# A triangle multiplication and a gated pair layer on one core: opening, first pair and drain laid out anew

## The chip, the cores and the metric

The kernel runs on one core of a Trainium2 chip, in one launch. The metric is the device time of a whole execution in microseconds. Engines are called by their short names: PE (TensorE, matmuls and transposes), DVE (VectorE), ACT (ScalarE), POOL (GpSimd) and SP (the queue from which most transfers are issued).

## The reference

x is 384 x 384 x 128 in fp32. Two layers follow each other; `_linear(x, W, b)` multiplies by the transposed W and adds b.

```python
# layer 0
z_n = _layernorm(z, norm_g, norm_b)
a = _linear(z_n, Wa, ba) * sigmoid(_linear(z_n, Wga, bga))
b = _linear(z_n, Wb, bb) * sigmoid(_linear(z_n, Wgb, bgb))
x = einsum('bijd,bjkd->bikd', a, b)
x = _layernorm(x, normo_g, normo_b)
z = z + _linear(x, Wo, bo) * sigmoid(_linear(z_n, Wgo, bgo))
# layer 1, with pair = z
left = pair @ W_left + b_left + (pair @ W_eq + b_eq)
right_sum = sum(pair @ W_right + b_right, axis=2)
gate = sigmoid(pair @ W_gate + b_gate)
out = (left * right_sum * gate) @ W_out + b_out
result = layer_norm(out + pair) * ln_scale + ln_bias
```

## The kernel before

The work goes in three stages.

**Stage 1** (about 0 to 1396 us) makes a, b and the output gate. It runs over 72 tiles n of 128 rows by 16 columns, each in four steps of four columns (`TS` is 4), 288 steps in all. A step s (`step`, L227) puts on PE the projections pga, pa, pgb, the transposes ptr of the next step (`turn`, L174), pb and the gate products pgo. ACT normalises columns to zn (L160), copies the transposed columns to zT (L191) and takes sigmoids; DVE takes the statistics of later columns (L141, L142) and forms at, bt and gs; POOL forms the factors of the norm (`norm_factors`, L144, whose power is L149), adds the bias to x for the residual (`residual`, L171) and issues the stores of a, of the gate and of the residual (A, G and Z in DRAM).

The opening stands ahead of the first step (L335 to L378). The first tile of x is fetched in four parts, the weights of layer 0 are fetched on ACT's queue (`weight`, L292), and `prepare` (L297) makes each weight ready: PE transposes it (L300), DVE copies it (raw, L302) and scales it by norm_g (L304), and a product of raw with norm_b is added to the bias (L309, L310, or L306, L307 for the gate of the output, "go"). `first_quarter` and `normalise` work on the first tile four columns at a time. `last_weights` (L313) prepares the weight of the output and a few constants of layer 1; it is a generator that goes one piece further after each step from s = `CATCH_UP`, which is 12.

The last columns of b stay in SBUF as b_held and are stored to B in pieces at the beginning of stage 2 (`store_held`, L539).

**Stage 2** (about 1396 to 2147 us) forms, for each of 128 channels d and three blocks ib of 128 rows, the product pm of a and b over 384 (`multiply`, L549, L554). Five of these products are begun early (`EARLY`, L577), before the last third of b is there. For each product DVE subtracts the first channel (xd, L566), ACT squares, DVE sums the squares (L547), POOL sums xd (L573), and SP stores xd into X. The last eight channels (`LAST`) are held in SBUF and run block by block, so that the deviation of one block (`deviation`, L455, a generator: variance, root, reciprocal, one Newton step, and `turn_factors` at L480) can go on beside the products of the next block. In the last block, `layer_0` is done for the rows u = 0 and 1 behind the third-last and the second-last product.

**Stage 3** (about 2147 to 3331 us) goes over the 384 rows u. The order within a turn of the loop is written out as a tuple of stages, each with a lag in rows: load, gate_product 3, turn 2, out_weights 7, layer_1 8, layer_0 0, norm_factors 12, normalise 13, project 2, last_right 2, store 17. Four rows (`R`) share a group: one norm of layer 1 on POOL and one store. A row puts on PE py (L437), ptr (L632), pleft and pg (L684, L686) and pf (L658); pf needs h from DVE and w_o, which is W_out scaled on ACT by the sums of that row (L640). The deviation of the last block runs on POOL beside the first rows (`last_deviation`, L485). The last rows pass through the same stages with nothing behind them; the store of the last eight is scaled on DVE (L709, L710) and issued row by row.

PSUM has eight banks; in stage 3 py, pf and pleft have two each, ptr and pg one each.

Of the kernel before, what the change touches and what calls it, by code (L numbers as in the profile page):

```python
# [1 line left out]

# [17 lines left out]
def kernel(ctx: ExitStack, tc: tile.TileContext, ins, out: bass.AP):  # L20
# [82 lines left out]
    with tc.tile_pool(name="wprep", bufs=6) as wp, tc.tile_pool(name="p1s", bufs=3) as ps, tc.tile_pool(  # L103
# [40 lines left out]
        def norm_factors(n, c0=0, c1=CX):  # L144
            if n >= NT:
                return
            mv, rstd, off = (tiles[n][k][:, c0:c1] for k in ("mv", "rstd", "off"))
            nc.gpsimd.tensor_scalar(rstd, mv[:, :, 1], EPS, None, ALU.add)
            nc.gpsimd.tensor_tensor(rstd, rstd, mhalf[:, 0 : c1 - c0], ALU.pow)  # L149
            nc.gpsimd.tensor_tensor(off, mv[:, :, 0], rstd, ALU.mult)  # L150
            nc.gpsimd.tensor_scalar(off, off, -1.0, None, ALU.mult)  # L151
            if c0 == 0:
                tiles[n]["zn"] = px.tile([P, CX, C], FP, tag="zn", name=f"zn_{n}", bufs=2)
# [20 lines left out]
        def turn(s):  # L174
# [4 lines left out]
            for c in range(CT):  # L179
                nc.tensor.transpose(ptr[:, c, :], tiles[n]["zn"][:, t * CT + c, :], ident)  # L180
            turned[s] = ptr
# [115 lines left out]
        def prepare(k):  # L297
            both = ppp.tile([P, CT, P], FP, tag="pk", name="w_" + k)
            pt, pb = both[:, 0, :], both[:, 1, :]
            nc.tensor.transpose(pt, wT[k], ident)  # L300
            raw = wp.tile([P, P], FP, tag="raw", name="raw_" + k, bufs=2)
            nc.vector.tensor_copy(raw, pt)  # L302
            scaled = ctile([P, P], "wT_" + k)
            nc.vector.tensor_scalar(scaled, raw, ng, None, ALU.mult)  # L304
            if k == "go":
                nc.tensor.matmul(pb, lhsT=nb_w, rhs=raw, start=True, stop=True)  # L306
                nc.vector.tensor_tensor(gate_bias, pb, gate_bias, ALU.add)  # L307
            else:
                nc.tensor.matmul(pb[:, 0:1], lhsT=raw, rhs=nb, start=True, stop=True)  # L309
                nc.vector.tensor_tensor(bcol[k], pb[:, 0:1], bcol[k], ALU.add)  # L310
            wT[k] = scaled

        def last_weights():  # L313
# [3 lines left out]
            pt = ppp.tile([P, CT, P], FP, tag="pk", name="pt_o")[:, 0, :]  # L317
            nc.tensor.transpose(pt, wT["o"], ident)
            raw, scaled = (wp.tile([P, P], FP, tag="raw", name=k + "_o", bufs=2) for k in ("raw", "scaled"))
            nc.vector.tensor_copy(raw, pt)  # L320
            nc.vector.tensor_scalar(scaled, pt, og, None, ALU.mult)
# [6 lines left out]
            nc.tensor.matmul(both[:, 1, :], lhsT=ob_w, rhs=raw, start=True, stop=True)  # L328
# [9 lines left out]
        for k in ("ga", "a", "gb", "b", "go"):  # L338
            weight(k, nc.scalar)
        nc.scalar.activation(warm, mhalf, AF.Sigmoid)  # L340
        ng, nb = column(L0 + "norm_g"), column(L0 + "norm_b")
        for k in ("ga", "a", "gb", "b"):
            bcol[k] = column(L0 + "b" + k)
            if k in ("a", "b"):
                next(x_parts)
# [18 lines left out]
        first_quarter(0)  # L364
        normalise(0, 0)
        prepare("ga")
        prepare("a")
        turn(0)
        turned_out(0)
        first_quarter(1)  # L370
        normalise(0, 1)
        prepare("gb")
        prepare("b")
        first_quarter(2)
        nc.vector.tensor_copy(nb_w, nb.to_broadcast([P, P]))
        prepare("go")
        first_quarter(3)
        later = last_weights()  # L378
        for s in range(NT * TS):
            step(s)  # L380
            if s >= CATCH_UP:
                next(later, None)
# [72 lines left out]
    def deviation(ib):  # L455
# [4 lines left out]
        v, t, r, sg, sd = (work(k) for k in ("v", "t", "r", "sg", "sd"))  # L460
# [7 lines left out]
        yield  # L468
        nc.scalar.activation(t, r, AF.Square)
# [4 lines left out]
        nc.vector.tensor_tensor(sd, v, r, ALU.mult)  # L474
        nc.sync.dma_start(out=X[ib][0], in_=sd)
# [8 lines left out]

    def last_deviation(ib, bank):  # L485

        v, t, r = (work_of.tile([P, N], FP, tag="w" + k, name=f"{k}_{ib}") for k in "vtr")
# [23 lines left out]
    with tc.tile_pool(name="p2", bufs=1, side="right", reuse_waits="tile") as p2, tc.tile_pool(  # L511
# [11 lines left out]
        order = [d for k in range(C // HELD) for d in range(k, C, C // HELD)]  # L523
# [15 lines left out]
        def store_held(i):  # L539
            if i < C:  # L540
                k = i // HELD
                nc.sync.dma_start(out=B[k :: C // HELD, N - P :, N - CG :], in_=b_held[k :: C // HELD])
# [37 lines left out]
        store_held(0)  # L580
# [4 lines left out]
        store_held(HELD)  # L585
        for d, ib in EARLY:
            multiply(d, ib, range(NB - 1))
        for d in range(C - LAST):
            fetch(d + AHEAD)
            if (d + 2) % HELD == 0:  # L590
                store_held(d + 2 + HELD)
# [8 lines left out]
        behind = None  # L600
        for ib in range(NB):
            for d in range(C - LAST, C):
# [8 lines left out]
                if ib == NB - 1 and d in (C - 3, C - 2):  # L611
                    layer_0(d + 3 - C, -1, lambda u: pp2.tile([P, N], FP, tag="pm", name=f"py_{u}").rearrange(
                        "p (q c) -> p q c", q=NB
                    ))
            add_squares()
            behind = deviation(ib) if ib < NB - 1 else None
# [4 lines left out]
    with tc.tile_pool(name="p3s", bufs=4, reuse_waits="tile") as ps, tc.tile_pool(  # L621
        name="p3g", bufs=4, reuse_waits="tile"
    ) as pg3, tc.tile_pool(name="p3y", bufs=2, space=PSUM, reuse_waits="tile") as pyp, tc.tile_pool(
        name="p3p", bufs=1, space=PSUM, reuse_waits="tile"
    ) as pp:
        hs, wos = {}, {}

        def turn(u):
            g, i = of(u)
            ptr = pp.tile([P, N], FP, tag="ptr", name=f"ptr3_{u}")  # L630
            for q in range(NB):
# [137 lines left out]
```

## Time and profile before

| What | us |
|---|---|
| Median of 3 runs | 3332.29 (3332.16 to 3332.49) |
| Profiled execution, its own time | 3332.67 |
| Its span, first to last instruction | 3330.9 |
| PE busy | 3289.1 (99%) |
| DVE busy | 2661.4 (80%) |
| ACT busy | 2309.9 (69%) |
| POOL busy | 2178.3 (65%) |
| Step of stage 1, usual period | 4.77 |
| Row of stage 3, usual period | 3.00 |

All times in the text are microseconds from the beginning of the span of this one execution, unless a line says otherwise. In lines of the timeline the first number is the start and the second the duration; a group in brackets at the end tells how long the engine stood idle before the instruction and what ended that.

### The profile page before, as it was taken

The numbers are of one execution on the slowest core, as the hardware profiler recorded it, in microseconds if no ns is written. First come the engines' busy times: TensorE is split into PE (matmuls) and PEld (weight loads), VectorE is DVE, ScalarE is ACT, GpSimd is POOL, SyncE is SP. The second block draws the span as 40 slices with busy tenths as digits, with TensorE's granted clock in tenths as the row PEclk, the third lists the DMA queues.
The fourth block names the chain that finished last, engine by engine and source line by source line (L and its number), as shares of the span: only waits on it lengthen the run. The fifth ranks groups of instructions, "written<-read, shape, count | busy, mean of one in ns | idle before, by whom it ended". The sixth has DMA issues, their size and how long they took to land.

```text
span 3330.9 us, 53440 instructions
## 1 busy us (share of the span) xinstructions
PE 3289.1 (99%) x15581; PEld 2188.5 (66%) x15581; DVE 2661.4 (80%) x8593; ACT 2309.9 (69%) x5485; POOL 2178.3 (65%) x1628
## 2 busy tenths in 40 slices
PE   8999999999999999999999999999999999999997
PEld 5555555555555555555555555588888888888885
DVE  8877777777777777555555555799999999999998
ACT  7777778787878788622222222388888888888887
POOL 6555555555555555355555555579999988888887
PEclk9999999999999999999999999999999999999998
DMA  6889899888988888899999999767777777777773
GB/s 224 266 256 273 277 281 281 280 276 281 285 275 270 256 273 279 276 347 310 318 312 311 312 312 304 262 238 266 266 264 261 261 260 262 262 264 263 262 264 143
DMA packets 675523, 910.52 MB, mean 273 GB/s; under 512 B 319521, under 2 KB 616481, under 8 KB 647713
## 3 DMA queue, kind: packets, MB, share of 16 engines
q1 hardware_dynamic: 634192, 680.28, 63.2%
q0 software_dynamic: 40320, 226.51, 19.4%
q8 instruction: 126, 2.06, 0.2%
q14 instruction: 165, 1.34, 0.1%
q10 hardware_dynamic: 720, 0.33, 0.0%
HBM read 454.04 MB, written 452.98 MB: 272 GB/s over the span
## 4 chain that ended last, share of the span: by engine, by line
PE 97%; DVE 1%; POOL 1%; ACT 0%; DMA 0%; issue 0%; POOLq 0%; ACTq 0%; DVEq 0%
PE pm L554 22%; PE py L437 8%; PE pf L658 8%; PE pga L246 8%; PE pleft L684 7%; PE pg L686 7%; PE pa L246 7%; PE pgb L246 7%; PE pb L246 7%; PE pgo L211 7%; PE ptr L632 4%; PE ptr L180 4%; PE pg L697 0%; DMA G<-gt 0%; POOL rs L667 0%
## 5 line engine op out<-in xcount | busy, mean ns | idle before, releaser
L554 PE MATMUL pm<-ab 128*128 128x384 f32 x2304 | 744.1, 486 | 1.5 <-DVE gs L213 1.5
L554 PEld LDWEIGHTS pm<-ab 128*128 128x128 f32 x2304 | 437.3, 190 | 306.4 <-DVE gs L213 2.7
L573 POOL TENSOR_TENSOR acc<-acc,xd 128x384 f32<-128x384 f32 x381 | 380.6, 999 | 362.7 <-DVE xd L566 362.7
L571 ACT ACTIVATE sq<-xd 128x384 f32<-128x384 f32 x381 | 188.5, 495 | 545.6 <-DVE xd L566 545.5
L276 DVE SCALAR_TENSOR_TENSOR bt<-pb,c_L_conv_bb,sgb 128x512 f32<-128x512 f32 x288 | 320.6, 1113 | 244.1 <-ACT zT L191 218.8
L160 ACT ACTIVATE zn<-xt,off,rstd 128x128 f32<-128x128 f32 x1152 | 503.3, 489 | 2.9 <-POOL off L151 2.8
L676 ACT ACTIVATE res<-res,off,rs 128x128 f32<-128x128 f32 x1152 | 482.3, 486 | 14.3 <-POOL off L670 11.4
L566 DVE TENSOR_TENSOR xd<-pm,acc 128x384 f32<-128x384 f32 x381 | 212.1, 557 | 340.9 <-POOL acc L573 321.3
L267 POOL DMA_DIRECT2D A<-at x72 | 85.5, 1188 | 538.8 <-DVE at L263 538.8
L443 DVE SCALAR_TENSOR_TENSOR py<-py,acc,gr 128x128 f32<-128x128 f32 x1152 | 395.9, 344 | 2.3 <-PE py L437 1.6
L251 ACT ACTIVATE sga<-pga,c_L_conv_bga 128x512 f32<-128x512 f32 x288 | 198.0, 687 | 266.7 <-PE pga L246 266.6
L211 PEld LDWEIGHTS pgo<-wT_go,zT 128*128 128x128 f32 x2176 | 285.7, 192 | 130.0 <-issue 66.5
L716 POOL TENSOR_TENSOR res<-res,r_L_conv_ln_bias 128x1536 f32<-128x1536 f32 x94 | 324.7, 3454 | 7.4
L171 POOL TENSOR_TENSOR acc<-xt,r_L_conv_b_out 128x2048 f32<-128x2048 f32 x72 | 327.7, 4552 | 1.8
L658 PE MATMUL pf<-w_o,h 128*128 128x128 f32 x2304 | 321.2, 276 | 6.1 <-ACT w_o L640 5.3
L691 ACT ACTIVATE sg<-pg,c_L_conv_b_gate 128x384 f32<-128x384 f32 x384 | 223.2, 581 | 148.2 <-PE pg L686 97.0
L715 POOL TENSOR_TENSOR res<-res,r_L_conv_ln_scale 128x1536 f32<-128x1536 f32 x94 | 325.0, 3458 | 0.1
L448 DVE BATCH_NORM_STATS2 st<-res 128x6 f32<-128x128 f32 x1152 | 323.7, 282 | 0.3
L437 PE MATMUL py<-w_o,xr 128*128 128x128 f32 x2304 | 320.7, 275 | 0.0
L684 PE MATMUL pleft<-pairT,m_L_conv_W_left 128*128 128x384 f32 x768 | 312.6, 489 | 1.8 <-ACT pairT L634 1.8
L686 PE MATMUL pg<-pairT,m_L_conv_W_gate 128*128 128x384 f32 x768 | 310.5, 486 | 0.0
L141 DVE BATCH_NORM_STATS2 st<-xt 128x6 f32<-128x128 f32 x1152 | 305.4, 265 | 3.7 <-DMA xt<-in_x_dram 3.7
(149 smaller groups left out, 6856.5 us busy)
## 6 DMA issues: line engine op xcount, KB each, us to landing
A<-at POOLq DMA_DIRECT2D x72, 1024.0 KB, 8.6
Z<-acc POOLq DMA_DIRECT2D x72, 1024.0 KB, 8.2
G<-gt POOLq DMA_DIRECT2D x72, 1024.0 KB, 8.7
gr<-G SPq DMA_DIRECT2D x96, 768.0 KB, 5.7
zr<-Z SPq DMA_DIRECT2D x96, 768.0 KB, 7.1
xr<-X SPq DMA_DIRECT2D x96, 768.0 KB, 8.3
X<-xd SPq DMA_DIRECT2D x381, 192.0 KB, 6.0
xt<-in_x_dram SPq DMA_DIRECT2D x71, 1024.0 KB, 17.1
```

Source lines behind the costliest of these rows:

```text
L160: nc.scalar.activation(g["zn"][:, c, :], g["x"][:, c, :], AF.Identity, bias=g["off"][:, c : c + 1], scale=g["rstd"][:, c : c + 1],)
L171: nc.gpsimd.tensor_tensor(zb, tiles[n]["x"], over(b_out, CX), ALU.add)
L211: nc.tensor.matmul(pgo[:, c, :], lhsT=zT[:, c, :], rhs=wT["go"], start=True, stop=True)
L246: nc.tensor.matmul(pk, lhsT=wT[k], rhs=zT, start=True, stop=True)
L437: nc.tensor.matmul(py[:, q, :], lhsT=g["x"][:, i, q * P : (q + 1) * P], rhs=w_o0, start=True, stop=True)
L443: nc.vector.scalar_tensor_tensor(py[:, q, :], py[:, q, :], rs0[:, q, u : u + 1], g["g"][:, i, q, :], ALU.mult, ALU.mult)
L554: nc.tensor.matmul(products[d, ib], lhsT=ab[:, 0, q, ib * P : (ib + 1) * P], rhs=ab[:, 1, q, :], start=(q == 0), stop=(q == NB - 1),)
L573: nc.gpsimd.tensor_tensor(s1[:, ib, :], s1[:, ib, :], xd, ALU.add)
L658: nc.tensor.matmul(pf[:, q, :], lhsT=h[:, q * P : (q + 1) * P], rhs=w_o, start=True, stop=True)
L676: nc.scalar.activation(g["res"][:, i, q, :], g["res"][:, i, q, :], AF.Identity, bias=g["off"][:, i, q : q + 1], scale=g["rs"][:, i, q : q ...
L684: nc.tensor.matmul(pleft, lhsT=w_left, rhs=pairT, start=True, stop=True)
L686: nc.tensor.matmul(pg[:, 0:N], lhsT=w_gate, rhs=pairT, start=True, stop=True)
```

## The change

It touches four places.

The opening. The host lays the weights of layer 0 out transposed, so `prepare` goes. `scale_weight` scales each weight by norm_g on ACT; the products with norm_b go into one bank, `biases`, and the biases of the four projections are added on ACT. The weight "go" is fetched on POOL's queue, and the second part of x is fetched ahead of most of the bias columns. `norm_factors` forms the negative mean ahead of the power, and for the first four columns its first two operations are on DVE. `keep_busy` puts transposes of the identity on PE, 32 in all, into a bank `idle` that nothing reads. `last_weights` starts at step 24 instead of 12, without its transpose.

The held columns of b. The first piece of 16 planes is stored as two of 8.

From products to rows. `layer_0` of rows 0 and 1 comes one product earlier, and row 0 is transposed behind the last product but one. The second half of block 1's deviation becomes `rest_of_deviation`, with one operation on ACT and four on POOL, in the first rows of stage 3. PSUM pools of stage 3 are named apart, with the same banks.

The drain. The loop over rows ends at u = 383, and what is left is written out in an order of its own. For the last four rows the residual is added on PE. The root of the last two groups' norm is taken on ACT with one Newton step on DVE. The last six rows are normalised into PSUM and scaled and shifted from there on DVE.

```diff
         def norm_factors(n, c0=0, c1=CX, beside=nc.gpsimd):
-            nc.gpsimd.tensor_scalar(rstd, mv[:, :, 1], EPS, None, ALU.add)
+            beside.tensor_scalar(rstd, mv[:, :, 1], EPS, None, ALU.add)
+            beside.tensor_scalar(off, mv[:, :, 0], -1.0, None, ALU.mult)
             nc.gpsimd.tensor_tensor(rstd, rstd, mhalf[:, 0 : c1 - c0], ALU.pow)
-            nc.gpsimd.tensor_tensor(off, mv[:, :, 0], rstd, ALU.mult)
-            nc.gpsimd.tensor_scalar(off, off, -1.0, None, ALU.mult)
+            nc.gpsimd.tensor_tensor(off, off, rstd, ALU.mult)
...
+        def scale_weight(k):
+            raw[k], wT[k] = wT[k], ctile([P, P], "wT_" + k)
+            nc.scalar.activation(wT[k], raw[k], AF.Copy, scale=ng)
...
-        for k in ("ga", "a", "gb", "b", "go"):
+        for k in ("ga", "a", "gb", "b"):
             weight(k, nc.scalar)
+        weight("go", nc.gpsimd)
         nc.scalar.activation(warm, mhalf, AF.Sigmoid)
         ng, nb = column(L0 + "norm_g"), column(L0 + "norm_b")
         for k in ("ga", "a", "gb", "b"):
+            if k in ("ga", "gb"):
+                next(x_parts)
             bcol[k] = column(L0 + "b" + k)
-            if k in ("a", "b"):
-                next(x_parts)
...
+        def keep_busy(times):
+            for k in range(times):
+                nc.tensor.transpose(idle[:, k % CT, :], ident, ident)
...
+        keep_busy(10)
+        statistics(0, CT)
+        norm_factors(0, 0, CT, nc.vector)
+        nc.vector.tensor_copy(nb_w, nb.to_broadcast([P, P]))
+        biases = ppp.tile([P, CT, P], FP, tag="pk", name="biases")
+        for k in gated_and_not + ("go",):
+            scale_weight(k)
+        for n, k in enumerate(gated_and_not):
+            nc.tensor.matmul(biases[:, 0, n : n + 1], lhsT=raw[k], rhs=nb, start=True, stop=True)
+        nc.tensor.matmul(biases[:, 1, :], lhsT=nb_w, rhs=raw["go"], start=True, stop=True)
+        first_quarter(1)
         normalise(0, 0)
-        prepare("ga")
-        prepare("a")
-        turn(0)
+        keep_busy(12)
+        turn(0, lambda: keep_busy(2))
         turned_out(0)
-        first_quarter(1)
+        keep_busy(2)
+        for n, k in enumerate(gated_and_not):
+            nc.scalar.activation(bcol[k], biases[:, 0, n : n + 1], AF.Identity, bias=bcol[k])
         normalise(0, 1)
-        prepare("gb")
-        prepare("b")
         first_quarter(2)
-        nc.vector.tensor_copy(nb_w, nb.to_broadcast([P, P]))
-        prepare("go")
         first_quarter(3)
+        nc.vector.tensor_tensor(gate_bias, biases[:, 1, :], gate_bias, ALU.add)
...
-            if s >= CATCH_UP:
+            if s >= 2 * CATCH_UP:
                 next(later, None)
...
+        if rest:
+            nc.scalar.activation(sg[:, 0:16], mhalf, AF.Sigmoid)
+            rest += [v, t, r]
+            return
...
+    def rest_of_deviation(ib, v, t, r, bank):
+        nc.scalar.activation(t, r, AF.Square, scale=0.5**0.5)
+        nc.gpsimd.tensor_tensor(t, t, v, ALU.mult)
+        yield
+        nc.gpsimd.tensor_scalar(t, t, -1.0, 1.5, ALU.mult, ALU.add)
+        yield
+        nc.gpsimd.tensor_tensor(r, r, t, ALU.mult)
+        yield
+        nc.gpsimd.tensor_tensor(t, v, r, ALU.mult)
+        nc.sync.dma_start(out=X[ib][0], in_=t)
+        yield
+        turn_factors(ib, r, bank())
+        yield
...
+        pieces = [slice(0, C, 2 * C // HELD), slice(C // HELD, C, 2 * C // HELD)]
+        pieces += [slice(k, C, C // HELD) for k in range(1, C // HELD)]
...
-                if ib == NB - 1 and d in (C - 3, C - 2):
-                    layer_0(d + 3 - C, -1, lambda u: pp2.tile([P, N], FP, tag="pm", name=f"py_{u}").rearrange(
-                        "p (q c) -> p q c", q=NB
-                    ))
+                if ib == NB - 1 and d in (C - 4, C - 3):
+                    layer_0(d + 4 - C, -1, lambda u: bank2(f"py_{u}").rearrange("p (q c) -> p q c", q=NB))
+                if ib == NB - 1 and d == C - 2:
+                    turn(0, bank2("ptr3_0"), pairs_of.tile([P, N], FP, tag="pair", name="pairT_0"))
...
-        for u in range(2, N + stages[-1][1]):
+        for u in range(2, N):
...
+        def layer_1_summed(u):
+            results(u)
+            pf = bank(u)
+            h, w_o, pair = hs.pop(u), wos.pop(u), pairs.pop(u)
+            for q in range(NB):
+                nc.tensor.matmul(pf[:, q, :], lhsT=ident, rhs=pair[:, q, :], start=True, stop=False)
+                nc.tensor.matmul(pf[:, q, :], lhsT=h[:, q * P : (q + 1) * P], rhs=w_o, start=False, stop=True)
...
+        def last_factors(u):
+            g, _ = of(u)
+            few = pp.tile([P, 4, R, NB], FP, tag="ptr", name=f"few_{u}")
+            v, r, t, rs = (few[:, k] for k in range(4))
...
+            nc.vector.tensor_scalar(v, g["mv"][:, :, :, 1], EPS, None, ALU.add)
+            nc.scalar.activation(sd, v, AF.Sqrt)
+            yield
+            nc.vector.reciprocal(r, sd)
+            nc.vector.tensor_copy(r_, r)
+            nc.vector.scalar_tensor_tensor(t_, r_, -0.5, r, ALU.mult, ALU.mult)
+            nc.vector.tensor_tensor(t, t_, v, ALU.mult)
+            nc.vector.scalar_tensor_tensor(rs, t, 1.5, r_, ALU.add, ALU.mult)
+            nc.vector.tensor_copy(rs_, rs)
+            nc.vector.scalar_tensor_tensor(off, g["mv"][:, :, :, 0], -1.0, rs, ALU.mult, ALU.mult)
+            g["rs"], g["off"] = rs_, off
+
+        def normalise_to_bank(u):
...
+            for q in range(NB):
+                nc.scalar.activation(
+                    banks[u][:, q, :], source[:, q, :], AF.Identity,
+                    bias=g["off"][:, i, q : q + 1], scale=g["rs"][:, i, q : q + 1],
+                )
+
+        def scale_and_shift(u):
+            g, i = of(u)
+            res = g["res"][:, i]
+            nc.vector.tensor_tensor(banks[u], banks[u], over(ln_s, NB), ALU.mult)
+            nc.vector.tensor_tensor(res, banks[u], over(ln_b, NB), ALU.add)
+            nc.sync.dma_start(out=y_out[u].rearrange("(p q) c -> p q c", q=NB), in_=res)
+
+        norm_factors(D - 12)
+        turn_row(D - 2)
+        gate_product(D - 3)
+        out_weights(D - 7)
+        layer_1(D - 8)
...
+        for u in range(D - 3, D):
+            out_weights(u)
+        nc.scalar.activation(pg3.tile([P, 16], FP, tag="root", name="root", bufs=1), ident[:, 0:16], AF.Sqrt)
+        statistics(D - 5)
+        first = last_factors(D - 8)
+        normalise(D - 12)
+        advance(first)
+        gate_product(D - 1)
+        normalise(D - 11)
+        store(D - 12, 2)
+        for u in range(D - R, D):
+            layer_1_summed(u)
+        statistics(D - 4)
+        normalise(D - 10)
+        normalise(D - 9)
+        store(D - 10, 2)
+        advance(first)
+        for u in range(D - 3, D):
+            statistics(u)
+        normalise(D - 8)
+        normalise(D - 7)
+        store(D - 8, 2)
+        normalise_to_bank(D - 6)
+        second = last_factors(D - R)
+        advance(second)
+        scale_and_shift(D - 6)
+        advance(second)
+        normalise_to_bank(D - 5)
+        scale_and_shift(D - 5)
+        for u in range(D - R, D):
+            normalise_to_bank(u)
+            scale_and_shift(u)
...
-        a = _np.ascontiguousarray(inputs[name])
+        a = inputs[name]
+        a = _np.ascontiguousarray(a.T if name.startswith("L0_conv_W") else a)
```

## The prediction

> **What bounds the kernel now.** I read the busy time by stretch first, then TensorE's waits, then the timelines of the few places where it idles.
>
> ```profile
> core 0: us, PE busy (x) PEld busy (x) DVE busy (x) ACT busy (x) POOL busy (x), PEclk, DMA share, GB/s
> 0.00:20.00 20.00, 11.26 (x25) 5.85 (x26) 11.87 (x57) 6.07 (x12) 8.45 (x25) 1.00 0.66 200
> ...
> 60.00:100.00 40.00, 38.25 (x162) 22.46 (x161) 37.44 (x111) 30.58 (x65) 27.32 (x21) 1.00 0.68 249
> ...
> 1230.00:2250.00 1020.00, 1013.07 (x3641) 615.13 (x3640) 620.83 (x1457) 399.24 (x866) 537.47 (x495) 1.00 0.90 296
> ...
> 3300.00:3331.00 31.00, 7.75 (x42) 5.97 (x42) 20.66 (x66) 16.46 (x44) 20.94 (x13) 0.67 0.28 101
> ```
>
> PE is busy 3289.1 of 3330.9 us. Of the 41.8 us idle, 8.7 lie in the first 20, 1.75 in 60 to 100, 6.9 in 1230 to 2250 and 23.2 in the last 31. Only what happens there, or at a low clock, can be won without taking PE work away, and the change takes hardly any away. The waits name the places:
>
> ```profile
> PE pf L658 <- ACT w_o L640: 5.3, 3, 4.2
> PE ptr L632 <- DVE acc L547: 4.0, 1, 4.0
> PE w_ga L300 <- DMA w_ga<-in_L_conv_Wga_dram: 4.0, 1, 4.0
> PE pm L554 <- DVE gs L213: 1.5, 1, 1.5
> PE pga L246 <- DVE scaled_o L321: 1.0, 1, 1.0
> ```
>
> (Columns: total us, times, longest.) The first sits in the drain, the second between the products and the rows.
>
> **Opening.** These lines show more than idleness (start, duration, then the instruction):
>
> ```profile
> 12.03 0.45 PE L300 MATMUL w_go<-ident,w_go 128*128 128x128 f32 x1
> 14.33 0.79 PE L306 MATMUL w_go<-raw_go,nb_w 128*128 128x128 f32 x2 [1.85 <-DVE raw_go L302]
> 14.91 1.91 PE L246 MATMUL pga<-zT,wT_ga 128*128 128x512 f32 x2
> 20.52 1.02 PE L246 MATMUL pb<-zT,wT_b 128*128 128x512 f32 x2
> 22.27 1.02 PE L246 MATMUL pga<-zT,wT_ga 128*128 128x512 f32 x2
> ```
>
> zT of step 0 is ready at 10.32, but PE still has three weights to prepare, so the first pga starts at 14.91. It takes 1.91 us and a later one 1.02: the clock is low until about 20. Step 0 thus takes 7.36 us, step 1 takes 4.77.
>
> Removed: five PE transposes, five DVE copies (0.28) and five DVE scalings (0.29). Added: five ACT scalings, counted at 0.29 spacing (L640, the same form, follows so), four small ACT bias adds of about 0.2, and some 32 dummy transposes. On SP the second part of x is issued fourth instead of sixth, some 2.5 us earlier; the bias columns behind it land later, needed only by ACT after 10. On ACT's queue w_go is gone, which waited there until 3.88 and held the table load (1.28) to 4.25; scalings can start near 4.3 and end near 6.0. w_go goes by POOL's queue. No row shows so small a load there: landing 2.2 us after issue (w_go's row) gives 4.6, a megabyte store (8.2) gives over 9; I take 5.5. Nothing but the last scaling and one bias product queues behind it; late by 3 us it would hold back norm quarter 0 on ACT by about 1.5.
>
> New chain: statistics to 5.3, two tiny DVE operations 0.25, POOL pow 1.04, off 0.2: 6.8. Four zn (1.65) end at 8.5, four transposes with fillers between at about 10.4, zT 0.6: pga near 11.05 instead of 14.91. If the fillers and bias products have the clock up by then, step 0 takes 4.77 and the second pga starts at 15.8: gain 6.4. If the transposes still run slow (pga at 12.7) it is 17.5: gain 4.8. I take 5.6.
>
> Here a rule speaks against the change. The Trainium skill, "TensorE: Matmul & The Clock Gate", Part 4, says that a transpose does not count as PE-busy for the clock gate in the way a matmul does. Then the fillers bring nothing: pga at 12.7 cold, step 0 takes 7.36, the second pga at 20.1: gain 2.2. The rows: after 2147.13 the clock is up within 3.1 us with three transposes among the matmuls; no stretch of transposes alone is in the trace. Real bias matmuls are mixed in here too, so I keep 5.6 and leave 2.2 to a rival.
>
> What is late next: DVE waits for the second x tile, issued at 6.96 and landing 8.3 later, 15.2; then at_0 16.7, gs_0 18.9, and PE wants gs_0 from 20.8. There are 2 us of slack.
>
> **Weights of the output.** At step 12, `last_weights` puts ob_w on DVE; it takes 4.40 us beside POOL's residual (L171, 80.17 to 84.71), while its sibling nb_w took 0.19. Groups pgo start at 73.81 and 95.68: four steps in 21.87, where 4 x 4.765 = 19.06: 2.8 us lost. The change takes a transpose and a copy out and starts it at step 24, where POOL's residual lies at 139.28 to 143.82 and gs at 139.80, so ob_w is blocked again, but with other slack: I count 0.75 + 0.44 (two products) + 0.75 = 2.0 lost. Gain 0.8 (0 to 2.8).
>
> **Held b.** The first pieces are 8 planes instead of 16. PE's cover is the early products (20 x 0.32 = 6.5 us, 1398.9 to 1404.1 after the 1.5 us wait for gs, which stays). The third they lead to lands about 1397 by my count: 7 us ahead of need. I cost it at 0; if that cover is gone it is worth up to the 1.5 us wait. One more SP issue of some 0.5 us counts against it: -0.5 to +1.5.
>
> **From products to rows.**
>
> ```profile
> 2140.69 1.17 DVE L474 TENSOR_TENSOR sd<-v,r 128x384 f32<-128x384 f32 x1
> 2141.78 1.13 DVE L443 SCALAR_TENSOR_TENSOR py<-py,acc,gr 128x128 f32<-128x128 f32 x3
> ```
> ```profile
> 2142.62 0.49 PE L482 MATMUL pr<-ident,r 128*128 128x128 f32 x3
> 2147.13 0.90 PE L632 MATMUL ptr<-ident,pair 128*128 128x128 f32 x3 [4.02 <-DVE acc L547]
> 2149.11 1.28 PE L684 MATMUL pleft<-pairT,m_L_conv_W_left 128*128 128x384 f32 x2
> 2152.26 0.91 PE L684 MATMUL pleft<-pairT,m_L_conv_W_left 128*128 128x384 f32 x2 [0.24 <-ACT pairT L634]
> ```
>
> DVE is the late one: second half of the deviation (L470 0.56, L472 1.17, L474 1.17) stands among the last products and two pairs; PE waits 4.0 and then runs cold (ptr 0.90 instead of 0.49, pleft 1.28 instead of 0.81). The change sends those three to ACT and POOL during rows 2 to 6, forms the first pair one product earlier and turns it before the products end. The x rows that pair_0 needs are issued at 2127.99 and land 4.3 later, in time for a product earlier. By my count pair_0 is ready at 2139.3, turned at 2140.7; PE ends the products at 2143.0, has pleft_0 at 2143.6 and pleft_1 at 2146.8 instead of 2152.26: gain 5.46. To pay: pr of the moved part in row 6 (0.4). ACT's added Square and POOL's four operations (0.83 to 1.17 each, L488 to L494) come where POOL had the last deviation, which moves five rows of its first turns later and is first needed at row 256; the moved store of sd on SP is needed at row 128. Table load L691 (1.28) moves ahead to a place where ACT idles. Taken 5.0, range 4 to 6.
>
> **Drain.** POOL's pow holds the last chain: 2.56 us at 3318.05, off until 3321.77, then
>
> ```profile
> 3321.80 4.73 ACT L676 ACTIVATE res<-res,off,rs 128x128 f32<-128x128 f32 x12 [6.19 <-POOL off L670]
> ```
>
> and DVE ends at 3327.72; the store and end take 3.2 more. The change adds the residual on PE (12 more matmuls), takes the last two groups' root on ACT and DVE (seven tiny operations, about 0.17 each), and normalises six rows into PSUM. From the same start: sg_383 3301.7, w_o to 3303.0 (the 4.2 us wait goes: its ACT queue had norm rows in front that waited for POOL), table load 1.28, row 372 and the root 3305.7, rows 373 to 377 at 1.16 to 3311.7, row 378 to 3313.2, 379 to 3314.8, factors 3315.6, four rows at 1.42 (three at 0.486 unoverlapped, since each writes the bank that the one before wrote) to 3321.3, DVE 1.1 more: 3322.5 instead of 3327.7. Gain 5.2 (3 to 7). ACT bounds it. POOL is late next: two rows at 3.45 a pair, done near 3320.3.
>
> A second rule against: "ScalarE: Activation LUTs", "What ACT_TABLE_LOAD costs", gives about 2.66 us a switch with its drain, where the load in this trace took 1.28. By the page the gain is 3.8; I take the trace.
>
> **Steady rows** keep their instructions, waits and bank count: 0.
>
> **Sum.** 5.6 + 0.8 + 0 + 5.0 + 5.2 = 16.6 us. The profiled execution took 3332.67 around its span of 3330.9, 0.4 above the median 3332.29. Span 3314.3, median 3315.7.
>
> **Rivals.**
> 1. The clock stays low in the opening (fillers don't count): opening 2.2, total 3319.1. For it: the rule. Against: matmuls among them.
> 2. The drain gives it back. ACT is the bound there, so the page's table load (+1.4) and slower in-bank rows (18 x 0.14 = 2.5 if each takes 0.63) leave 1.3: 3319.6. No row shows ACT writing PSUM in place.
> 3. The second x tile or w_go lands 3 us later than counted: opening 2.8, 3318.5.
> 4. Slower than before: pools and order of the row loop are rewritten around it. Rows take 3.00 us with PE at 2.96 and both PE and DVE busy throughout (929.3 and 929.4 of 930), so any new wait per row shows in full. Over 374 rows, 0.044 us a row eats 16.6; 0.06 gives 3338. Against: the same eight banks, and each row's waits are the same.
> 5. Better: all warm at 15.8, drain 7, boundary 6: about 3311.
>
> **How the numbers follow.** Forecast 0.52; rival 1 0.15; 2 0.15; 3 0.05; 5 0.07; so much failing that it stays within 0.2% 0.03; rival 4 0.03. A measurement of this kernel can tell about 0.2%, 6.7 us, from no change. Faster 0.94, same 0.03, slower 0.03. Range: upper end rivals 1 to 3 joined in part (3322), lower end rival 5 with last_weights at its best (3310).
>
> **What would show it.** In the profile after: first pga near 11 and at 1.02 rather than 1.91, the second near 16; a loss of about 2 us after step 24; no 4 us wait before the rows' first ptr and pleft_1 within 4 us of the last product; rows still 3.00; ACT unbroken from 3301 to 3321 less the shift, DVE's last operation 3 us before the end. A first step of 7 us, drain longer than 25 us after py_383, or rows above 3.02 would make it wrong.

## The result and the profile after

The changed kernel takes 3317.55 us (median of 6 runs, 3314.97 to 3319.84) where the kernel before takes 3332.39 beside it: a ratio of 0.9956, interval 0.9943 to 0.9969, or 14.8 us less. The forecast was 3315.7. The profiled execution is the fastest of the six: 3314.97 us, span 3313.2, which is 17.7 less than the span before; the sum of the prediction, made for a profiled execution, was 16.6.

Busy time of the engines by stretch, of the kernel after (stretch, length, then busy time of PE, PEld, DVE, ACT, POOL, PE's granted clock, DMA share, GB/s):

```profile
0.00:20.00 20.00, 17.08 (x77) 12.88 (x78) 11.91 (x54) 13.52 (x34) 9.45 (x26) 1.00 0.68 202
120.00:170.00 50.00, 49.38 (x208) 28.81 (x207) 42.01 (x120) 38.81 (x83) 26.16 (x22) 1.00 0.78 253
1230.00:2250.00 1020.00, 1017.02 (x3691) 619.98 (x3690) 625.42 (x1491) 405.17 (x886) 542.56 (x499) 1.00 0.91 298
3285.00:3314.00 29.00, 10.37 (x78) 9.11 (x76) 19.00 (x82) 21.03 (x54) 20.27 (x11) 0.76 0.33 120
```

The first 20 us now have PE busy for 17.08 instead of 11.26, though part of that is dummies. Steps 24 to 28 (120 to 170) have 0.6 us of idleness where steps 12 to 16 had 1.75, the stretch from 1230 to 2250 has 3.0 instead of 6.9, and the drain 18.6 instead of 23.2. The waits of PE in the same execution:

```profile
PE pleft L728 <- ACT pairT L467: 1.7, 5, 0.6
PE idle L358 <- POOL mhalf L61: 1.3, 1, 1.3
PE biases L370 <- DMA c_L_conv_norm_b<-in_L_conv_norm_b_dram: 1.3, 1, 1.3
PE pm L593 <- DVE gs L216: 0.8, 1, 0.8
```

The waits of 5.3 (pf for w_o), 4.0 (the rows' first ptr) and 4.0 (the first weight) have gone. What is left was there before too, belongs to the dummies, or is the wait of the new bias products for their column. A ledger from one place to the next, each read from the two timelines, gives the worth of each part:

| Place | before | after | gained since the place above | predicted |
|---|---|---|---|---|
| second pga starts | 22.27 | 16.65 | 5.62 | 5.6 |
| first product starts | 1395.93 | 1389.26 | 1.05 | 0.8 |
| second group of products starts | 1398.92 | 1391.54 | 0.71 | 0 |
| pleft of row 1 | 2152.26 | 2139.53 | 5.35 | 5.5 |
| last py (row 383) | 3293.65 | 3281.29 | -0.37 | -0.4 |
| DVE's last operation ends | 3327.72 | 3309.53 | 5.83 | 5.2 |
| end of the span | 3330.9 | 3313.2 | -0.5 | 0 |

The places, in the timeline of PE after:

```profile
11.78 1.12 PE L249 MATMUL pga<-zT,wT_ga 128*128 128x512 f32 x2 [0.24 <-ACT zT L194]
...
16.65 1.02 PE L249 MATMUL pga<-zT,wT_ga 128*128 128x512 f32 x2
...
1391.54 2.85 PE L593 MATMUL pm<-ab 128*128 128x384 f32 x8 [0.83 <-DVE gs L216]
...
2135.40 0.83 PE L443 MATMUL py<-w_o,xr 128*128 128x128 f32 x6
2136.36 0.88 PE L728 MATMUL pleft<-pairT,m_L_conv_W_left 128*128 128x384 f32 x2
...
2139.53 0.91 PE L728 MATMUL pleft<-pairT,m_L_conv_W_left 128*128 128x384 f32 x2 [0.65 <-ACT pairT L467]
```

The first pga runs warm (1.12 instead of 1.91), and between the products and the rows there is neither a long wait nor a cold matmul ("warm" and "cold" stand for PE's clock as the durations show it: projections follow each other every 0.86 us warm, and every 1.71 cold). The drain is the chain on ACT that was forecast, from the table load on:

```profile
3290.84 1.28 ACT L863 ACT_TABLE_LOAD   x1
3292.14 0.22 ACT L863 ACTIVATE root<-ident 128x16 f32<-128x16 f32 x1
3292.26 1.25 ACT L720 ACTIVATE res<-res,off,rs 128x128 f32<-128x128 f32 x3
3293.41 0.16 ACT L806 ACTIVATE sd<-few 128x12 f32<-128x12 f32 x1
3293.47 5.87 ACT L720 ACTIVATE res<-res,off,rs 128x128 f32<-128x128 f32 x15
3299.25 1.43 ACT L825 ACTIVATE end<-res,off,rs 128x128 f32<-128x128 f32 x3
3300.62 0.16 ACT L806 ACTIVATE sd<-few 128x12 f32<-128x12 f32 x1
3300.68 1.44 ACT L825 ACTIVATE end<-res,off,rs 128x128 f32<-128x128 f32 x3
3303.15 5.19 ACT L825 ACTIVATE end<-end,off,rs 128x128 f32<-128x128 f32 x12 [1.04 <-DVE off L814]
```

### The profile page after: what moved, and what is told of

The parts are those of the page before. It is cut to its first block, busy times and chain, and to the rows that moved or that the text cites. A ratio compares the mean times of both kernels' runs of the same rounds, so it can differ in the third digit from the quotient of the medians.

```text
span 3313.2 us, 53541 instructions
## 1 busy us (share of the span) xinstructions
PE 3287.9 (99%) x15631; PEld 2192.3 (66%) x15631; DVE 2652.2 (80%) x8585; ACT 2311.9 (70%) x5499; POOL 2176.8 (66%) x1627
## 4 chain that ended last, share of the span: by engine, by line
PE 98%; ACT 1%; DMA 0%; DVE 0%; issue 0%; SPq 0%; ACTq 0%; DVEq 0%
PE pm L593 22%; PE pf L702 8%; PE py L443 8%; PE pga L249 8%; PE pleft L728 7%; PE pg L730 7%; PE pb L249 7%; PE pgb L249 7%; PE pa L249 7%; PE pgo L214 7%; PE ptr L466 4%; PE ptr L181 4%; PE pg L741 0%; DMA G<-gt 0%; ACT res L720 0%; ACT end L825 0%
## 5 line engine op out<-in xcount | busy, mean ns | idle before, releaser
L720 ACT ACTIVATE res<-res,off,rs 128x128 f32<-128x128 f32 x1134 | 474.7, 486 | 3.4 <-POOL off L714 1.2
L449 DVE SCALAR_TENSOR_TENSOR py<-py,acc,gr 128x128 f32<-128x128 f32 x1152 | 451.8, 392 | 0.9
L454 DVE BATCH_NORM_STATS2 st<-res 128x6 f32<-128x128 f32 x1128 | 374.3, 332 | 0.0
L751 POOL TENSOR_TENSOR res<-res,r_L_conv_ln_bias 128x1536 f32<-128x1536 f32 (+1 forms) x96 | 326.7, 3403 | 7.5
L750 POOL TENSOR_TENSOR res<-res,r_L_conv_ln_scale 128x1536 f32<-128x1536 f32 (+1 forms) x96 | 326.9, 3405 | 0.8 <-ACT res L720 0.5
```

The lines of the kernel that those rows point to most:

```text
L449: nc.vector.scalar_tensor_tensor(py[:, q, :], py[:, q, :], rs0[:, q, u : u + 1], g["g"][:, i, q, :], ALU.mult, ALU.mult)
L454: nc.vector.bn_stats(b["st"][:, k, q, :], b["res"][:, k, q, :])
L720: nc.scalar.activation(g["res"][:, i, q, :], g["res"][:, i, q, :], AF.Identity, bias=g["off"][:, i, q : q + 1], scale=g["rs"][:, i, q : q ...
```

## The experiments

Two questions were left by so close a result: do the parts gain for the reasons given, and why does the kernel now vary by 5 us from run to run where the one before stays within about 2? e1 to e4 were timed beside 23 runs of the kernel before (median 3332.74), e5, e7, e8 and e10 beside 12 others (3332.41), and e6, e9, e11 and e12 beside another 12 (3332.96).

### The dummies in the opening, and the spread (e1, e2, e3)

e1 is the changed kernel once more. e2 leaves every `keep_busy` out. e3 fills the hole ahead of the bias products:

```diff
-        keep_busy(10)
+        keep_busy(16)
...
-        keep_busy(12)
+        keep_busy(8)
```

Expected of e1: 

> The changed kernel once more, unaltered, to see what varies: six runs of it lay between 3315.0 and 3319.8 us, where the kernel before stays within 1.1 us. Theory A (the clock in the opening comes up a varying time after the first dummy transposes): every place from the third step on keeps its distance to the next one, and a slower profile has its second pga later than 16.65 us by the whole difference, up to 20. Theory B (transfers or the drain vary): second pga at 16.6 to 16.7 in any profile, and the difference appears between the last products and the end. Times within 3315 to 3320 again.

Expected of e2: 

> The changed kernel without its 32 dummy transposes. If they bring the clock up (theory A): the first pga comes near 10.7 but runs at 1.9 us, step 0 takes about 7.3, the second pga near 18, so 1.5 to 3 us slower than with them. Rival (transposes do not count for the clock gate): the bias products and the real matmuls set the clock, nothing is lost and the 12 that delay the first real transposes by 1.1 us are saved: second pga near 15.5, 1 us faster.

Expected of e3: 

> The changed kernel with 16 dummy transposes first instead of 10 and 8 instead of 12 before the first real ones: the hole of 1.34 us before the bias products is filled. Theory A: the clock is up by 6, the bias products take 0.2 instead of 0.42 each, first pga near 10.7 and second near 15.5, so 1 us faster in the profile, and the spread over runs falls to that of the kernel before (1 us), which makes the median some 3 us better than the changed kernel's. Rival (the hole does not matter): same as the changed kernel, same spread.

Measured: e1 3317.28 us (3316.00 to 3320.42), e2 3315.19 (3314.98 to 3316.86), e3 3316.02 (3315.55 to 3318.26). Without any dummy the kernel is no slower. PE's timeline of e2:

```profile
7.88 1.63 PE L181 MATMUL ptr<-ident,zn 128*128 128x128 f32 x4 [0.21 <-ACT zn L161]
10.18 2.07 PE L249 MATMUL pga<-zT,wT_ga 128*128 128x512 f32 x2 [0.67 <-ACT zT L194]
...
13.75 1.53 PE L249 MATMUL pgb<-zT,wT_gb 128*128 128x512 f32 x2
...
17.31 1.02 PE L249 MATMUL pga<-zT,wT_ga 128*128 128x512 f32 x2
```

Cold projections cost e2 over 2 us, but its first ptr starts at 7.88, as soon as zn is there. In the changed kernel it starts at 9.85, because twelve dummies stand before it at half speed. The profiled run of the changed kernel has its second pga 0.66 us earlier than e2 (16.65 against 17.31), but it is the earliest of eight profiles with that opening: the others, from e1, e4, e6, e7, e8, e9 and e11, lie between 16.99 and 17.86. So the dummies bring nothing that can be told from the spread.

Do transposes count for the clock, then? e3 answers, where 16 of them run from 1.35 to 4.68 and nothing else does:

```profile
3.75 0.93 PE L358 MATMUL idle<-ident 128*128 128x128 f32 x5
5.27 0.35 PE L370 MATMUL biases<-c_L_conv_norm_b,w_ga 128*128 128x1 f32 x2 [0.59 <-DMA c_L_conv_norm_b<-in_L_conv_norm_b_dram]
...
14.84 1.02 PE L249 MATMUL pga<-zT,wT_ga 128*128 128x512 f32 x2
...
20.35 1.12 PE L249 MATMUL pga<-zT,wT_ga 128*128 128x512 f32 x2 [0.59 <-ACT zT L194]
```

The first bias product takes 0.35 us where it took 0.56, so the clock was up by 5.3 after transposes alone. The rule that the prediction weighed (Part 4 of "TensorE: Matmul & The Clock Gate" in the Trainium skill) does not hold here. The second pga comes 1.8 us earlier than in the changed kernel, and 0.75 of that is given back at once: the third waits for zT.

But the clock does not come up at one time. Read from the durations, it is up by 9.85 in the changed kernel, near 11.4 in e8 and 12.4 in e6, which have the same opening, and near 12.9 in e12, whose dummies are those of e3 (first two lines below). In e10, again with those dummies, it was up for the bias products and down again for the first real transposes (last two lines), until about 11:

```profile
5.49 0.56 PE L373 MATMUL biases<-c_L_conv_norm_b,w_ga 128*128 128x1 f32 x2 [0.46 <-DMA c_L_conv_norm_b<-in_L_conv_norm_b_dram]
12.48 1.22 PE L249 MATMUL pga<-zT,wT_ga 128*128 128x512 f32 x2
```

```profile
5.55 0.35 PE L371 MATMUL biases<-c_L_conv_norm_b,w_ga 128*128 128x1 f32 x2 [0.82 <-DMA c_L_conv_norm_b<-in_L_conv_norm_b_dram]
7.83 0.42 PE L181 MATMUL ptr<-ident,zn 128*128 128x128 f32 x1
```

The granted clock of the profile shows 1.00 throughout, so it is no help there. Part 1 of the same page ("The HAM clock gate") says that the gate looks at a window that runs freely and does not start with the kernel; a varying release fits that, though no run here shows the window itself. The clock is not alone in moving the opening: in the eight profiles the first bias product starts between 5.08 and 5.79, as its columns land, and e1, the latest, owes its second pga of 17.40 to that (it comes 11.61 after the first bias product, against 11.57 in the changed kernel):

```profile
5.79 0.55 PE L370 MATMUL biases<-c_L_conv_norm_b,w_ga 128*128 128x1 f32 x2 [2.04 <-DMA c_L_conv_bga<-in_L_conv_bga_dram]
```

The second varying place is the end of stage 1. Seven profiles with the same code up to there (the changed kernel, e1, e4, e7, e8, e9, e11) have a wait before the second group of products of 0.6 to 2.4 us. ACT's timeline of the changed kernel says what it hangs on:

```profile
1388.34 2.19 ACT L201 ACTIVATE gt<-gs 128x512 f32<-128x512 f32 x4 [4.60 <-DMA G<-gt]
```

The kernel before has the same there (ACT's and PE's timelines):

```profile
1395.72 2.19 ACT L198 ACTIVATE gt<-gs 128x512 f32<-128x512 f32 x4 [5.31 <-DMA G<-gt]
1398.92 3.35 PE L554 MATMUL pm<-ab 128*128 128x384 f32 x9 [1.54 <-DVE gs L213]
```

ACT may fill a gate tile only when the store of an earlier one has landed; DVE's gs and PE's PSUM bank queue behind it. In all seven, in e3, in e6 and in the kernel before, the second group starts 3.20 us after ACT goes on, whenever the first product was (in e7, with the longest wait, ACT goes on at 1390.26). So the landing of that store sets the start of stage 2, and what PE wins earlier is lost in this wait unless the store lands earlier too: in e3 the first product is 0.93 us ahead of the changed kernel's, but ACT goes on at 1388.36 and the second group starts at 1391.56. Both theories of e1 thus hold in part. The two places together move the second group between 1391.5 and 1393.5 in the seven. Executions above 3319 us were not caught in a profile of this kernel, so the rest of their time stays open.

e2 differs from the changed kernel in a second way. The bank `idle` came from the same six banks in turn as the products of stage 1, so without it other banks fall to the early products. ACT goes on late in e2 as well (1389.05), but PE does its first three groups without a wait, and from ACT's going on to pleft of row 1 it takes 750.69 us instead of 751.19. e5 and e12 below, which take `idle` from the other pool, have 750.65 and 750.64. The order of banks is the likely reason for these 0.5 us; it was not tried apart.

### The opening alone (e4)

The kernel before with the opening of the changed one. 

> The kernel before with the new opening alone (with last_weights from step 24). By the ledger of the two profiles this is worth 5.6 us to the second pga and 1.05 us more to the end of stage 1: 3325.7 in a run like the profiled one, and with a spread of 5 us over runs if theory A holds (3325 to 3331); within 1 us if the spread is made in the drain.

Measured: 3327.51 us (18 runs, 3326.04 to 3330.78), 5.2 less than before. The second pga is at 17.57 in its profile, the first product at 1390.21 and the second group at 1392.49. Of the 18 runs 17 lie within 2.3 us (the 23 of the kernel before: within 2.0), and one stands apart at 3330.78. So the opening and the end of stage 1 make part of the changed kernel's spread of 5 us, but they are not shown to make most of it. Another part lies outside the span: the time of an execution exceeds its span by 1.72 to 1.83 us in every run of e4, of e2 and of the kernel before beside these experiments, but by 1.72 to 2.86 in the eleven of the changed kernel. What makes up to 1.1 us of difference there is open.

The parts add up: 5.2 for e4, 4.98 for the boundary and 5.3 for the drain (from the ledger) make 15.5, where the changed kernel's two medians are 14.8 and 15.5 below the kernel before.

### Taking what e3 gave back (e5, e12, e10)

e5 is e3 with `idle` taken from the other PSUM pool and the second tile of x in parts:

```diff
-        gate_bias = rows(L0 + "bgo")
-        fetch(1)
+        for _ in fetch_parts(1, TS):
+            pass
+        gate_bias = rows(L0 + "bgo")
```

e12 moves that row behind the first part. e10 is e5 with three buffers (`bufs=3`) for the gate tiles.

Expected of e5: 

> The changed kernel with the hole before the bias products filled (16 and 8 dummy transposes, as in the run before of that kind), and with the second x tile fetched in four parts ahead of the bias row; the bank of the dummies comes from the other PSUM pool. In the filled version the second pga started at 14.84 but the third waited for zT until 20.35, because DVE's statistics waited for the whole second tile. If that landing is what gave the gain back: third pga at 19.6 and no wait on zT, 0.8 us kept. If instead ACT or the norm on POOL is late: third pga still later than 20. For the end of stage 1: if the wait at the first products hangs on the landing of the gate's store (G), the second group of products starts no earlier than in the changed kernel (distance to the third pga longer by what was won); if it follows the DVE queue, the win stays. Median 3314.5 if it stays, 3316 if not.

Expected of e12: 

> The version with the hole filled and the second x tile in parts, now with the bias row of the gate fetched behind the first part instead of behind the fourth; there DVE waited for that row until 14.75, so the third pga was no earlier than with the whole tile. Theory: DVE does the first part's statistics near 13, at_0 by 14.5, third pga at 19.6 without a wait, 1 us earlier than the filled versions; what of it lasts beyond stage 1 depends on the store of G, whose landing DVE's gs waits for at the end: at best 1 us (median 3314.4), at worst nothing (3315.4). Rival: ACT's eight zn between sga and sgb are late anyway (third pga 20.2 or later).

Expected of e10: 

> The same, with three buffers instead of two for the tiles of the output gate that are stored to G. Theory: at the end of stage 1 DVE's gs waits for ACT's gate, and that for the store of an earlier gate tile; with a third buffer the wait of PE before the second group of products (0.83 to 1.77 us in the profiles so far) is gone: 1 us faster than the run beside it, median about 3313. Rival: gs is late for DVE's own queue or the products wait for the transfers of A and B that are issued only when stage 1's stores are out: same as beside it.

Measured: e5 3315.43 us (3314.18 to 3316.23), e12 3315.46 (3314.29 to 3316.52), e10 3323.32 (3321.15 to 3325.54). In e5 the third pga is at 20.61: DVE stood until 14.75 for the gate's bias row, now behind four transfers. In e12 DVE has at_0 at 15.17, but the clock came up late (second pga 17.44), so whether the third could be at 19.6 was not seen. Their waits before the products sum to 0.8 and 0.3. e5, e12 and e2 have the lowest medians measured, about 2 us below the changed kernel, with ranges that overlap its own; among themselves they can't be told apart. As e2 shares neither the filled hole nor the parts of the tile with the other two, the gain can't be put down to these; what the three share is that `idle` does not come from those six banks, which goes with the 0.5 us above. The rest is open.

e10 shows the store's part: with a third buffer PE's wait on gs is gone, and a larger one takes its place:

```profile
PE pm L594 <- DMA ab<-B: 7.7, 1, 7.7
```

The first loads of stage 2 are issued later: the fourth pair at 1382.21 instead of 1357.24, the held piece of b at 1383.62 instead of 1376.38. The likely reason is the 8 KB a partition for the third buffer, which the first factors had used; that was not tried apart.

### Where the weights of the output are prepared (e6)

```diff
-            if s >= 2 * CATCH_UP:
+            if s >= CATCH_UP:
```

> The changed kernel with last_weights from step 12, as before, without its transpose. Read from the distances between pga of one step and another, which vary by under 0.1 us. In the changed kernel steps 24 to 28 take 20.66 instead of 19.06, a loss of 1.6; before, steps 12 to 16 lost 2.8. Theory (ob_w is held by POOL's residual wherever it starts, and the place decides how much of that PE sees): steps 12 to 16 lose 2.2 to 2.7, steps 24 to 28 none, 1 us slower to the end of stage 1. Rival (the removed transpose and copy made the difference): loss 1.6 at step 12 too, no difference.

Measured: pga of step 12 at 70.28 and of step 16 at 91.82, a loss of 2.48 us; steps 24 to 28 lose nothing. The kernel before loses 2.81, the changed one 1.60. So 0.33 is due to the transpose and copy left out and 0.88 to the place: ob_w takes 4.35 us on DVE at step 12 and 3.45 at step 24 (the lines of e6 and of the changed kernel), PE's wait for at is 1.26 and 0.38.

```profile
75.97 4.35 DVE L306 COPY ob_w<-c_L_conv_normo_b 128x128 f32<-128x128 f32 x1
```

```profile
131.97 3.45 DVE L306 COPY ob_w<-c_L_conv_normo_b 128x128 f32<-128x128 f32 x1
```

3318.51 us in all, within the spread of the changed kernel.

### Held b (e9)

The first piece again of 16 planes. 

> The changed kernel with the first held piece of 16 planes instead of two of 8. The prediction costs the smaller pieces at nothing, because the early products cover the last third of B: no wait of PE on that transfer, the same distance from the second group of products to the first pleft (744.8 us) within 0.1. Rival (the smaller piece brings the third in time): a wait of PE on the fetch of B of up to 1.5 us and a longer distance.

Measured: 744.82 us from the second group to the first pleft in e9 and in the changed kernel alike, and no wait on B. The smaller pieces are worth nothing here. 3316.45 us, within the spread.

### The boundary: DVE's load or the earlier pair (e8)

```diff
-            behind = (deviation(ib), deviation(ib, rest), None)[ib]
+            behind = (deviation(ib), deviation(ib), None)[ib]
...
-            rest_of_deviation(*rest, lambda: pfp.tile([P, N], FP, tag="pf", name="pr_1")),
```

> The changed kernel with the whole deviation of block 1 back on DVE behind the products of block 2, while the pairs of rows 0 and 1 stay one product earlier. This parts the two halves of the change at the boundary. If DVE's load decides (three operations, 2.9 us), pleft of row 1 comes 2.5 to 3 us later after the last product than in the changed kernel (4.13 after the py that closes the products) and the table load falls between; about 2.5 us slower in all, 0.4 given back by the absent transposition in row 6. If the earlier pair decides alone: within 0.5 us of the changed kernel.

Measured: from the second group of products to pleft of row 1 750.93 us, where the changed kernel has 747.99 and the one before 753.34. The moved half of the deviation is worth 2.94, the earlier pair and transposition 2.4. That half is DVE's three operations, their transposition on PE, and the earlier table load on ACT, which the edit moves along. From there to the last py e8 is 0.35 quicker, the price of the transposition in row 6. 3319.63 us in all. Its waits of PE name the engine that is late again:

```profile
PE py L443 <- DVE pair L456: 0.8, 1, 0.8
PE ptr L466 <- DVE pair L456: 0.8, 1, 0.8
```

```profile
2144.35 0.91 PE L728 MATMUL pleft<-pairT,m_L_conv_W_left 128*128 128x384 f32 x2 [0.69 <-ACT pairT L467]
```

### The drain: PSUM, and the root (e7, e11)

e7 writes the last six rows into `g["res"]` (SBUF) instead of the banks, and scales them there. e11 takes the roots of the last two groups from POOL (`norm_factors`, the second ahead of a store) and leaves out `last_factors`, with the table load.

Expected of e7: 

> The changed kernel with the last six rows normalised into SBUF instead of PSUM, and scaled there. On ACT a row into PSUM took 1.43 against 1.25 us for three into SBUF, so ACT alone would win 0.8 us. Theory: the detour by PSUM is there because DVE's two-operand operations in SBUF stand behind POOL's stores, which run until 3306 in the drain (before: L709 took 2.57 instead of 0.56 beside POOL). Then L833 or L834 show 1.5 to 3 us in places, the second root's factors on DVE come 2 us later, and the drain is 1 to 3 us longer. Rival (no such block): 0.8 us shorter, all these operations at 0.56.

Expected of e11: 

> The changed kernel with the root of the last two groups back on POOL as a power (2.3 us with 0.7 around it), each issued as soon as its statistics are there and ahead of the next store on POOL; ACT's root, its table load and DVE's small operations are gone. Theory (POOL's queue set the drain before): POOL is busy with stores without a gap from 3288 to 3306, so each power adds its 3 to 4 us to that queue, ACT waits for off twice, and from the last py to DVE's end it takes 31 to 34 us instead of 28.2, as before (34.1). Rival (ACT is the bound, and loses the table load of 1.28 and the two roots): 26.7 to 28.

Measured from the last py to DVE's end: 30.32 us in e7, 30.80 in e11, 28.24 in the changed kernel, 34.07 before. e7 takes 3319.38 us in all. Its ACT is quicker as expected (four rows 4.30 instead of 5.19), yet DVE is held up beside POOL (the timelines of DVE and of POOL):

```profile
3303.09 2.04 DVE L833 TENSOR_TENSOR res<-res,r_L_conv_ln_bias 128x384 f32<-128x384 f32 x1
```

```profile
3302.72 2.00 POOL L751 TENSOR_TENSOR res<-res,r_L_conv_ln_bias 128x768 f32<-128x768 f32 x1
```

The operation took 0.56 from PSUM, beside the same stores of POOL, and 0.56 from SBUF in e7 once POOL was done. Counted from the last py, the second factors come 1.3 us later than in the changed kernel, and the next rows with them. e11 takes 3324.12 us: ACT waits for POOL twice,

```profile
3300.51 2.41 ACT L720 ACTIVATE res<-res,off,rs 128x128 f32<-128x128 f32 x6 [3.25 <-POOL off L714]
...
3307.51 5.19 ACT L825 ACTIVATE end<-end,off,rs 128x128 f32<-128x128 f32 x12 [1.88 <-POOL off L714]
```

and the span ends 7.8 us after DVE, not 3.7. SP's queue tells why: the six row stores stand behind the last store of POOL's,

```profile
3297.15 18.01 SPq L752 DMA_DIRECT2D out_dram<-res  x4
3315.25 3.14 SPq L835 DMA_DIRECT2D out_dram<-res  x6
```

and POOL is done only at 3314.76. The changed kernel has the same order:

```profile
3306.74 3.15 SPq L835 DMA_DIRECT2D out_dram<-res  x6
```

The row stores begin when POOL's last store has gone out, though the first row was ready at 3301.9. The last of them is issued 0.1 us behind DVE's end, as before, but these stores of 192 KB take 2.5 us to land (median), where those before took 1.9. The likely reason is that the six now follow close on each other; that fits the 0.5 us by which the end of the span lies further behind DVE's last operation. Another order on SP was not tried.

## Why the prediction held

**Opening.** The total was right (5.62 for 5.6) with luck, its inside only in part. The other seven profiles with this opening would give 4.4 to 5.3, nearer to the prediction's slow case (second pga at 17.5, gain 4.8). The first pga came at 11.78 instead of 11.05, since the dummies ran slow longer than thought; step 0 was warm. The rival "clock stays low" was mis-sized: it kept the twelve dummies in the way and let the whole of step 0 run cold (20.1, gain 2.2), while with no dummies at all the second pga is at 17.31, a gain of 4.96. Nearly all of the gain is the work taken out or moved ahead of the first step, and not the dummies; its pieces were not parted. DVE's wait for the second tile was called the next late thing, with 2 us of slack; with a gain of 1.8 more (e3) it was.

**Output weights.** 1.2 us by the steps (2.81 to 1.60) for 0.8; the 2.0 of loss counted for step 24 was 1.6.

**Wait before the products.** The prediction let 1.5 us stay and got 0.8, which is luck: other profiles of the same code have up to 2.4. The term missed was the landing of G's store, which moves from run to run and, by its fixed 3.20 us to the second group, decides how much of an earlier first product is kept. Held b at nothing was right (e9). Its cover was mis-stated: 1398.9 to 1404.1 is 5.2 us, the 16 of the 20 early products that follow the wait; the margin of 7 us stands.

**Boundary.** 5.35 and -0.37 for 5.46 and -0.4, and by the mechanism named (e8). It repeats: 747.99 us from the second group to pleft of row 1 in e1, e7, e9 and e11 too.

**Drain.** ACT's chain fell within 0.35 us of its forecast times up to the second factors, counted from the last py. Rows in place in PSUM took 0.43 us an operation (5.19 for twelve) instead of the 0.486 assumed: that is most of the 0.6 that DVE ended earlier. The switch of tables cost 1.28 with nothing ahead of it or behind it (w_o ends at 3290.82, the next operation starts at 3292.14), so the 2.66 us of the Trainium skill ("ScalarE: Activation LUTs", What ACT_TABLE_LOAD costs) does not show here. The order of SP's queue was overlooked: POOL's end was named as the next late thing, not that the row stores are queued behind it.

**Rows.** 1141.39 and 1141.76 from pleft of row 1 to the last py, with the 0.4 paid: no change per row.

**The measured median** gained 2.9 less than the profile, because the profiled execution was the best of six; the prediction saw no spread in the change. As its sum was also 1.1 too low for that execution, the two errors partly cancel, and its centre lay only 1.9 low. (Of its rivals, the fifth has a slip: its own parts make about 3312, not 3311.)

## What to carry to other kernels

Dummy work to raise PE's clock belongs only where PE would idle anyway: here, put ahead of the first real instruction at half speed, it delayed by 2 us what it was to speed up. Split a profile into stretches by fixed places and give each part of a joined change its own difference; that shows what adds up and what is given back. Read the same places in several profiles before calling a part exact: the opening and the end of stage 1 moved by 1 to 2 us, the boundary not at all. When a late engine is relieved, look at the queue behind it next: here a store's landing and a bias row each took the next turn.

## What the runs showed of the hardware beside that

- TensorE's clock came up after 16 transposes of the identity and nothing else, by 5.6 us in three runs (e3, e5, e10) and not before 12 in a fourth (e12) with the same dummies; in e10 it was down again at 7.8 and up near 11.
- DVE's add of 128x384 in SBUF took 2.04 us beside a POOL operation and 0.56 from PSUM, with POOL's own going from 1.80 to 2.00.
- ACT's normalise of 128x128 came every 0.38 us into SBUF and every 0.43 in place in PSUM.
